# A 3x3 convolution rewritten as F(4,3) over rows and five products per two outputs over columns

## The chip, the cores and the metric

One core of a Trainium2 chip runs the whole program. The metric is device time in microseconds (us). Every figure "median" is over several executions; a profile is one execution, recorded instruction by instruction.

TensorE does matmuls (PE in the profile, PEld its weight loads), VectorE (DVE) and ScalarE (ACT) work element by element, GpSimd is POOL, SP issues transfers. SBUF and PSUM are the core's memories; the kernels' products land in PSUM.

## The reference

Two bottleneck blocks, one after the other, on 64 images of 1024 x 14 x 14, all float32:

```python
out = relu(bn(conv(x, w1, b1, 1, 0)))      # 1x1, 1024 -> 256
out = relu(bn(conv(out, w2, b2, 1, 1)))    # 3x3, 256 -> 256, padding 1
out = bn(conv(out, w3, b3, 1, 0))          # 1x1, 256 -> 1024
out = relu(x + softplus(residual_scale) * out)
```

`bn` takes mean and variance over all images and pixels, so each convolution must be finished for all images before its result can be normalised. That makes stages: 1x1, 3x3, a Gram stage (it gets the statistics of the third convolution from the second moments of its input), then the last 1x1 together with the next block's first.

## The kernel before

The 3x3 convolution is direct. Per two images the normalised activations go into a zero-padded tile, and each of two output halves is the sum of 18 products (2 input halves x 9 taps) of 392 columns:

```python
def conv2(t, w2, par, aff, stats):
    ...                                    # pad <- relu(scale * y + shift), ScalarE
    for o in range(MS):                    # 2 output halves
        ps = psum_tile()
        for s in range(MS):                # 2 input halves
            for k, (i, j) in enumerate(TAPS):
                nc.tensor.matmul(ps..., w2[:, s, k, o, :], pad[:, s, :, i : i + H, j : j + W],
                                 start=..., stop=...)
        y = ys[t][:, o, :]
        nc.scalar.activation(y, ps, AF.Identity, bias=...)      # PSUM -> SBUF
        nc.vector.bn_stats(stats[:, o, t, :], y)
...                                        # cut
for t in range(T):                         # T = 32 pairs of images
    conv2(t, w2, pb, aff, stats2)
aff = affine(aggregate(stats2, MS), MS, pb, G2, BE2)
grams = gram(aff, crow)                    # norm, transposes, Gram products
```

## Time and profile before

| | us |
|---|---|
| median of the kernel before | 3131.7 |
| TensorE busy (profiled run, span 3130.5) | 3088.2 |
| 3x3 products, both blocks | 1520.9 |
| 1x1 products, all | 1367.9 |
| VectorE busy, all stages | 563.9 |

The 1x1 figure is 681.2 + 686.7 from the two groups. The point to read from the table: one engine is busy for 99% of the span, and the direct 3x3 products are half of that. The column "mean ns" of a matmul group is how long one matmul is in flight; its cost in a stream is the distance from start to start, which is shorter.

### The profile page before, as it was taken

The numbers are of one execution on the slowest core, as the hardware profiler recorded it, in microseconds if no ns is written. First come the engines' busy times: TensorE is split into PE (matmuls) and PEld (weight loads), VectorE is DVE, ScalarE is ACT, GpSimd is POOL, SyncE is SP. The second block draws the span as 40 slices with busy tenths as digits, with TensorE's granted clock in tenths as the row PEclk, the third lists the DMA queues.
The fourth block names the chain that finished last, engine by engine and source line by source line (L and its number), as shares of the span: only waits on it lengthen the run. The fifth ranks groups of instructions, "written<-read, shape, count | busy, mean of one in ns | idle before, by whom it ended". The sixth has DMA issues, their size and how long they took to land.

```text
span 3130.5 us, 23038 instructions
## 1 busy us (share of the span) xinstructions
PE 3088.2 (99%) x10032; PEld 1845.2 (59%) x10032; DVE 563.9 (18%) x998; ACT 636.5 (20%) x1039; POOL 42.4 (1%) x76
## 2 busy tenths in 40 slices
PE   8999999999999999999999999999999999999998
PEld 5555555555555577555555555555555555875554
DVE  1111100000000033223222321000000000334444
ACT  1111111011111051223222321111101100524444
POOL 0000000000000000000000000000000000000000
PEclk9999999999999999999999999999999999999999
DMA  6444000000000021434344332000000000027886
GB/s 250 160 145 164 14 0 0 0 0 1 0 0 0 0 93 42 165 144 157 152 152 157 144 124 96 0 1 0 0 1 0 0 0 0 1 104 306 295 295 254
DMA packets 36581, 267.60 MB, mean 85 GB/s; under 512 B 2688, under 2 KB 2944, under 8 KB 27520
## 3 DMA queue, kind: packets, MB, share of 16 engines
q1 hardware_dynamic: 22592, 160.96, 14.4%
q0 software_dynamic: 13312, 102.76, 8.0%
q10 hardware_dynamic: 576, 2.40, 0.2%
q8 instruction: 79, 1.29, 0.2%
q14 instruction: 22, 0.18, 0.0%
HBM read 163.35 MB, written 102.76 MB: 85 GB/s over the span
## 4 chain that ended last, share of the span: by engine, by line
PE 59%; issue 39%; POOL 1%; DMA 1%; DVE 0%; POOLq 0%; ACT 0%; SPq 0%; ACTq 0%
PE ps L120 24%; PE ps L99 21%; PE ps L132 11%; PE g L151 1%; PE ps L163 1%; PE g L152 1%; POOL out L229 1%; DMA x<-mid 0%; DMA x<-in_x 0%; PE ps L209 0%; PE ps L206 0%; PE ps L197 0%; PE ps L199 0%; PE ps L198 0%; POOLq L229 0%
## 5 line engine op out<-in xcount | busy, mean ns | idle before, releaser
L120 PE MATMUL ps<-pad,w 128*128 128x392 f32 x4608 | 1520.9, 493 | 10.3 <-ACT pad L111 10.3
L120 PEld LDWEIGHTS ps<-pad,w 128*128 128x128 f32 x4608 | 872.5, 189 | 658.7 <-ACT pad L111 11.5
L99 PE MATMUL ps<-x,w 128*128 128x392 f32 x2048 | 681.2, 493 | 10.4 <-DMA x<-in_x 10.4
L132 PE MATMUL ps<-y,w 128*128 128x392 f32 x2048 | 686.7, 496 | 0.0
L99 PEld LDWEIGHTS ps<-x,w 128*128 128x128 f32 x2048 | 390.0, 190 | 295.9 <-issue 11.9
L132 PEld LDWEIGHTS ps<-y,w 128*128 128x128 f32 x2048 | 391.9, 192 | 286.6 <-issue 4.7
L227 ACT ACTIVATE x<-x,shift 128x392 f32<-128x392 f32 x512 | 318.2, 621 | 381.0 <-DVE x L224 381.0
L224 DVE SCALAR_TENSOR_TENSOR x<-ps,scale,x 128x392 f32<-128x392 f32 x512 | 320.3, 626 | 336.1 <-PE ps L132 332.4
L127 DVE BATCH_NORM_STATS2 stats<-y 128x6 f32<-128x392 f32 x128 | 72.9, 569 | 1450.2 <-ACT y L126 1450.2
L126 ACT ACTIVATE y<-ps,par 128x392 f32<-128x392 f32 x128 | 75.1, 587 | 1048.0 <-PE ps L120 1048.0
L104 ACT ACTIVATE y<-ps,par 128x392 f32<-128x392 f32 x128 | 75.1, 587 | 575.6 <-PE ps L99 575.6
L105 DVE BATCH_NORM_STATS2 stats<-y 128x6 f32<-128x392 f32 x128 | 72.9, 570 | 614.5 <-ACT y L104 614.5
L111 ACT ACTIVATE pad<-y,shift,scale 128x392 f32<-128x392 f32 x128 | 90.1, 708 | 320.0 <-PE ps L120 316.7
L151 PE MATMUL g<-zt 128*128 128x257 f32 x392 | 119.7, 387 | 0.0
L165 DVE TENSOR_TENSOR zt<-ps,crow 128x512 f32<-128x512 f32 x98 | 67.9, 693 | 108.5 <-PE ps L163 108.3
L152 PEld LDWEIGHTS g<-zt 128*128 128x128 f32 x392 | 75.2, 192 | 11.4
L139 ACT ACTIVATE y<-y,shift,scale 128x392 f32<-128x392 f32 x128 | 77.7, 701 | 3.2 <-DVE shift L266 3.2
L152 PE MATMUL g<-zt 128*128 128x129 f32 x392 | 76.3, 277 | 0.0
L163 PE MATMUL ps<-ident,y 128*128 128x128 f32 x392 | 61.8, 282 | 10.4 <-issue 5.2
L151 PEld LDWEIGHTS g<-zt 128*128 128x128 f32 x392 | 60.6, 195 | 0.6 <-DVE zt L165 0.6
L163 PEld LDWEIGHTS ps<-ident,y 128*128 128x128 f32 x392 | 47.7, 146 | 12.8 <-ACT y L139 7.0
L229 POOL DMA_DIRECT2D mid<-x x32 | 17.2, 537 | 1864.2 <-ACT x L227 1864.2
(65 smaller groups left out, 125.2 us busy)
## 6 DMA issues: line engine op xcount, KB each, us to landing
x<-in_x SPq DMA_DIRECT2D x64, 1568.0 KB, 6.4
mid<-x POOLq DMA_DIRECT2D x32, 1568.0 KB, 5.4
x<-mid SPq DMA_DIRECT2D x32, 1568.0 KB, 7.7
out<-x POOLq DMA_DIRECT2D x32, 1568.0 KB, 7.8
w<-in_w SPq DMA_DIRECT2D x2, 2304.0 KB, 15.5
w<-in_w ACTq DMA_DIRECT2D x2, 1024.0 KB, 5.9
w<-in_w SPq DMA_DIRECT2D x2, 1024.0 KB, 14.3
par<-in_par ACTq DMA_DIRECT2D x2, 146.5 KB, 10.2
```

The source lines that it names most:

```text
L99: nc.tensor.matmul(ps.rearrange("p (i f) -> p i f", i=G), w1[:, s, o, :], xt[:, :, s, :], start=(s == 0), stop=(s == CS - 1),)
L104: nc.scalar.activation(y, ps, AF.Identity, bias=par[:, B1 + o : B1 + o + 1])
L111: nc.scalar.activation(pad[:, s, :, 1 : H + 1, 1 : W + 1], ys[t][:, s, :].rearrange("p (i h w) -> p i h w", i=G, h=H), AF.Relu, bias=shift ...
L120: nc.tensor.matmul(ps.rearrange("p (i h w) -> p i h w", i=G, h=H), w2[:, s, k, o, :], pad[:, s, :, i : i + H, j : j + W], start=(s == 0 an ...
L126: nc.scalar.activation(y, ps, AF.Identity, bias=par[:, B2 + o : B2 + o + 1])
L132: nc.tensor.matmul(ps, w3[:, s, o, :], ys[t][:, s, :], start=(s == 0), stop=(s == MS - 1))
L139: nc.scalar.activation(y, y, AF.Relu, bias=shift[:, s : s + 1], scale=scale[:, s : s + 1])
L151: nc.tensor.matmul(g0, zt[:, c, 0:P], zt[:, c, :], start=first, stop=last)
L152: nc.tensor.matmul(g1, zt[:, c, P:M], zt[:, c, P:], start=first, stop=last)
L163: nc.tensor.transpose(tp[:, (c * MS + s) * P : (c * MS + s + 1) * P], y_all[:, s, px], ident)
L224: nc.vector.scalar_tensor_tensor(v, ps.rearrange("p (i f) -> p i f", i=G), scale[:, o : o + 1], v, ALU.mult, ALU.add)
L227: nc.scalar.activation(v, v, AF.Relu, bias=shift[:, o : o + 1])
```

## The change

The intent is to do the 3x3 convolution with fewer multiplications. Over rows, F(4,3) turns four output rows, each with three taps, into six products of combined input rows with combined filters (six in place of twelve). Over columns, two neighbouring outputs take five products in place of six: one product of w1 with the sum of an even and an odd column serves both outputs. In exchange VectorE forms the row combinations and the column sums, and recombines products into output rows. The combined filters are made on the chip in the first stage, kept in DRAM and fetched per use. SBUF pools are opened and closed by stage to make room.

```diff
+GI = 8                          # images of one group
+BUFS = dict(u=3, t=3, r=4, sums=4, ms=3, f=2)
+    def combine(g, pair):        # rows of products (1,2), (3,4) or (0,5)
+            if pair[0] == 1:
+                ...              # t1, t2: four scalar_tensor_tensor, two edge rows on ScalarE
+                nc.vector.tensor_add(ra, t1, t2)
+                nc.vector.tensor_sub(rb, t1, t2)
+            ...                  # cut: the other two pairs
+            for i, r in zip(pair, (ra, rb)):
+                nc.vector.tensor_add(sums, r[:, :, :, WH:], r[:, :, :, :WH])
+                u = pool.tile([P, MS, NK, M], FP, tag="u", name="u", bufs=BUFS["u"])
+                nc.sync.dma_start(out=u, in_=us[b][i])
+    def products(made):
+            ...                  # per row combination i and output half o, s = 0, 1:
+                        nc.tensor.matmul(m[:, o, :n], w(s, D1D2), sums[:, s]...)
+                        nc.tensor.matmul(odd, w(s, D1), r[:, s, :, WH:], ...)
+                        nc.tensor.matmul(odd[:, :, : WH - 1], w(s, D3), r[:, s, :, WH + 1 :], ...)
+                        nc.tensor.matmul(even, w(s, D2), r[:, s, :, :WH], ...)
+                        nc.tensor.matmul(even[:, :, 1:], w(s, D0), r[:, s, :, : WH - 1], ...)
+                ...              # ms <- m, ScalarE
+    def columns(done):           # f <- PSUM + ms, VectorE
+    def finish(g, pair, done, acc):
+            ...                  # output rows from f, then eight bn_stats per group
+        for k, (g, pair) in enumerate(pairs):
+            if pair[0] == 1 and g + 1 < NG:
+                norm(g + 1, aff)
+            now, ahead = ahead, combine(*pairs[k + 1]) if k + 1 < len(pairs) else None
+            acc = finish(g, pair, products(now), acc)
-        for t in range(T):
-            conv2(t, w2, pb, aff, stats2)
```

The host packs pixels in another order (8 images together, even and odd columns apart); the 1x1 stages keep their matmuls.

## The prediction

> **What bounds the kernel now.** I read the page first (busy shares), then the chain that ended last in order of time, then busy time by stage, then the groups by shape, and last single stretches of the timeline for what one instruction costs.
>
> ```profile
> PE 3088.2 (99%) x10032; PEld 1845.2 (59%) x10032; DVE 563.9 (18%) x998; ACT 636.5 (20%) x1039; POOL 42.4 (1%) x76
> PEclk9999999999999999999999999999999999999999
> ```
> TensorE is busy for 99% of the span at full clock; nothing else is above 20%. A change pays only where it shortens TensorE's queue, and only until another engine fills up.
>
> The chain in order of time (start, length, what), around the first 3x3 convolution:
> ```profile
> 349.51 0.59 ACT y L104
> 350.13 0.58 DVE stats L105
> 350.73 1.03 DVE mv L238
> 353.88 0.72 ACT pad L111
> 354.65 760.69 PE ps L120 x2304
> 1115.34 5.21 issue
> ```
> The 3x3 convolution of one block is 760.7 us of matmuls without a hole, 330.2 ns each (760.69/2304), with some 5 us of TensorE idle before it and 5.2 after it. By stage (window: length, then busy time and count of PE, PEld, DVE, ACT, POOL, clock, DMA share, GB/s):
> ```profile
> 0.00:340.00 340.00, 329.64 (x996) 190.27 (x997) 37.94 (x89) 39.67 (x68) 2.59 (x12) 1.00 0.45 166
> 340.00:1110.00 770.00, 764.82 (x2318) 438.72 (x2317) 41.75 (x79) 81.59 (x131) 0.00 (x0) 1.00 0.01 2
> ```
> In the 3x3 stage VectorE works 42 of 770 us and the DMA rings are empty: room for both kinds of work that the change brings. The costs of one instruction (busy us in total, mean ns):
> ```profile
> L120 PE MATMUL ps<-pad,w 128*128 128x392 f32 x4608 | 1520.9, 493 | 10.3 <-ACT pad L111 10.3
> L111 ACT ACTIVATE pad<-y,shift,scale 128x392 f32<-128x392 f32 x128 | 90.1, 708 | 320.0 <-PE ps L120 316.7 <-DVE shift L266 3.3
> L139 ACT ACTIVATE y<-y,shift,scale 128x392 f32<-128x392 f32 x128 | 77.7, 701 | 3.2 <-DVE shift L266 3.2
> L152 PE MATMUL g<-zt 128*128 128x129 f32 x392 | 76.3, 277 | 0.0
> L105 DVE BATCH_NORM_STATS2 stats<-y 128x6 f32<-128x392 f32 x128 | 72.9, 570 | 614.5 <-ACT y L104 614.5
> L165 DVE TENSOR_TENSOR zt<-ps,crow 128x512 f32<-128x512 f32 x98 | 67.9, 693 | 108.5 <-PE ps L163 108.3
> ```
> Mean ns of a matmul is a latency; its cost is the step from start to start. There are 4608 records for 2304 products in the code: each float32 product is two instructions. In the chain, 32 of 392 columns take 10.53 us (329.1 ns each), the Gram pairs of 257 columns 0.44 us (220 each), and pairs of 512 columns 0.86. All fit columns x 0.8333 ns + 2.5 ns. The timeline shows whether the weight load sets a floor:
> ```profile
> 1215.45 3.66 PE L206 MATMUL ps<-zmean,w 128*128 128x2 f32 x32
> 1228.67 0.17 DVE L253 TENSOR_TENSOR q<-r 128x8 f32<-128x8 f32 x1
> 1228.87 0.17 DVE L254 TENSOR_TENSOR q<-q,v 128x8 f32<-128x8 f32 x1
> ```
> 32 matmuls of two columns need 3.49 us by the chain, 109 ns each, so a fresh 128x128 weight set can go in every 109 ns; the 189 ns printed for a weight load is latency too. The two VectorE lines depend on each other and step 0.20 us; independent ones elsewhere in that stretch step 0.07 to 0.12.
>
> **What the Trainium skill says.** "TensorE: Matmul & The Clock Gate", Back-to-back issue gap, gives columns/2.4 + 2.5 ns warm, and LDWEIGHTS columns/1.2 (107 ns). The trace agrees on the 2.5 and on the load (109), but a float32 instruction takes twice the slope. "VectorE: DVE Perf Modes", section on the TRN2 errata, has a float32 tensor_tensor at (N+151)/0.96 ns: 691 for 512, measured 693; two-tensor float32 operations get no faster mode. "ScalarE: Activation LUTs", What ACT_TABLE_LOAD costs, has 280 + 0.833 N ns with one pointer operand and 93 more for a second: 700 for 392 elements, measured 701. "PSUM — Partial Sum Buffer", Specifications, warns that any non-contiguous pattern "slows matmuls significantly"; all outputs of the kernel before are contiguous, so no run shows it yet.
>
> **The change, part by part** (per group of 8 images; 8 groups per block, 16 in all).
>
> TensorE, removed: 144 products of 392 columns, 1521.4/16 = 95.1 us. Added: six transformed rows, each for two output halves with ten products: six of 224 columns and four of 192 (lines of 7 columns, 32 lines; the edge products drop one of 7). That is 2 x 2112 columns; the sixth row has 24 lines, 2 x 1584. In all 5 x 4224 + 3168 = 24288 columns, against 56448. Two instructions each: 48576 x 0.8333 = 40.48 us, plus 240 x 2.5 ns = 0.60: **41.1 us**. The smallest, 144 columns, takes 122.5 ns, above the 109 ns floor, so weight loads do not bind. All 16 groups: 657 us.
>
> VectorE, added: I count elements and instructions in the code. Row combinations 4032 + 4032 + 3472 elements (24 instructions), column sums out of PSUM 5152 (12), output rows 1792 + 4928 + 1568, and statistics 3136 (20 together): 28112 elements, 56 instructions. At 0.96 per ns: 29.3 us. With 65 ns for each step that overlaps and about seven dependent steps at 130 more: 33.8 us. With every instruction at its full 160 ns and 40 ns to the next: 40.5 us. So VectorE is 82 to 98% of TensorE's 41.1: full, but below it.
>
> ScalarE: two norms of 1568 elements (373 + 1306 ns, 3.4 us), five edge rows (about 0.4 each), seven PSUM copies (0.45 to 0.57 each): about 9 us. Hidden.
>
> DMA: six filter tiles of 1.31 MB per group, 7.9 MB per 41 us = 191 GB/s; the last stage of the kernel before (2870 to 3130 us) moves 286. Of three buffers the current pair holds two; the second tile of the next pair can be fetched when the first row is done with its own (7.1 us of products) and is needed 14 us later, and a 1.57 MB tile lands in 6.4 us now. Hidden. Filter preparation: 4 x about 12 us of VectorE, 15.7 MB of stores, in the first stage, where VectorE is at 38 of 340 us: hidden.
>
> At the two edges of each block TensorE is idle longer. Entry: now one pad of 0.72 us after the shift; then two norms (3.3), edge rows (0.4), two of the first combinations after the second norm (0.9), the sum and difference (2.1) and the first column sum (0.5), 7.2: +6.5 us. Exit: now one eviction, one statistic, and a norm; then the last row's columns (1), two output rows (1.8), eight statistics (3.9), two norms instead of one (+2.5): about +9 us. Two blocks: +31. The other stages keep their matmuls: the 1x1 convolutions have the same columns in another pixel order, their reads and evictions in runs of 28 or more, and the input tiles become one contiguous run per partition. I give that nothing either way.
>
> Sum: 3132 - 1521 + 657 + 31 = 2299. The windows of three pairs are uneven: while TensorE runs the short pair (12.5 us), VectorE must finish the columns, differences and rows of the middle pair and combine the next group's first pair, 11.4 us by the lower count and over 13 by the upper. I allow 1.5 us of stall per group, 24 us, giving 2323; I say 2325.
>
> **Rivals.** (a) VectorE becomes the bound of the stage. For: 40.5 of 41.1 us in the upper count, six hand-overs a group, one queue in order. Against: independent steps overlap in the trace. At 45 us a group the stage is 720: about 2390. (b) Short runs slow the matmuls: operands in runs of 6 or 7, outputs of 6 out of 7. For: the skill's warning. Against: runs of 14 in the input cost 330.2 against 329.1 ns here. If only the 16 shortened instructions per row took double, 16 x 162 ns x 6 x 16 = 250 us more: about 2570. (c) False waits between rows of the one big activation tile: ScalarE's norm of the next group (3.3 us) waiting for VectorE, and VectorE for it, once a group: +50, about 2375. (d) Weight tiles through DRAM arrive late: I see 1 to 2 us a tile at worst, 100 to 200 us more; the empty rings speak against it.
>
> **Range and chances.** The gain of 807 us rests on a TensorE rate measured to a per cent; a, c and half of b all push up, and almost nothing pushes below 2285 except the stall allowance and the edges being smaller. So the range is lopsided: 2285 to 2430. For a loss, the new stage would have to take over 95 us a group, more than twice the larger count; faster by over 2% 0.985, within 2% 0.01, slower 0.005.
>
> **What would show it.** After: 3840 instructions of the new products (240 x 16) in place of 4608; steps of about 189 ns (224 columns) and 162 (192) in the chain; a 3x3 stage of some 340 us with TensorE over 93% busy and VectorE at 80 to 95%; few waits of TensorE on the row combinations or on PSUM. If TensorE waits mostly on VectorE's sums, (a) holds; if 192-column steps exceed 165 ns, (b); if the filter tile releases it, (d). My prediction fails most simply if the overlap of VectorE instructions seen with 8 elements is not there with hundreds.

## The result, and the profile after

The changed kernel takes 2309.93 us in the median (4 runs, 2309.51 to 2311.61) against 3131.7 (3131.13 to 3132.34). The ratio is 0.7377, with a 95% interval of 0.7364 to 0.739. Ratios are the mean time of one kernel's fast runs over that of the other's of the same rounds, so they are not quite the ratio of the medians. The result is correct. The prediction was 2325, range 2285 to 2430.

The page of the changed kernel, busy time by engine and, in 40 slices, the clock granted to TensorE in tenths of full speed (PEclk; 9 is 90% or more):

```profile
PE 2236.0 (97%) x9264; PEld 1637.6 (71%) x9264; DVE 1077.3 (47%) x1854; ACT 581.4 (25%) x911; POOL 48.4 (2%) x102
PEclk9999998999998999999999999999999998999999
```

TensorE lost 852 us of work and is still busy for 97%. VectorE's work has nearly doubled. The clock now dips to 8 in three slices; the first two (346 to 404 and 692 to 750 us) hold the entry and the exit of the first 3x3 stage, which matters below.

The first block's 3x3 stage in three windows (length, then busy time and count of PE, PEld, DVE, ACT, POOL, clock, DMA share, GB/s): the entry, the products, the exit.

```profile
349.16:361.85 12.69, 0.01 (x2) 0.03 (x1) 8.59 (x21) 10.37 (x11) 0.00 (x0) 0.58 0.78 310
361.85:696.20 334.35, 334.35 (x1920) 331.76 (x1920) 260.72 (x430) 57.60 (x105) 0.00 (x0) 1.00 0.48 177
696.20:707.23 11.03, 0.03 (x1) 0.03 (x1) 8.55 (x22) 2.04 (x3) 0.20 (x4) 0.65 0.78 306
```

The middle line carries the answer: 1920 matmuls fill 334.35 of 334.35 us. VectorE is busy for 260.7 of them (78%), the DMA rings for half. The other two lines are the price: 12.7 and 11.0 us in which TensorE does nothing and VectorE and ScalarE, in turn, finish one stage and begin the next.

What TensorE waits for in the whole changed kernel (us in total, times, longest):

```profile
PE ps L334 <- ACT y L147: 23.6, 4, 11.0
PE ps L221 <- ACT t L161: 12.7, 1, 12.7
PE ps L221 <- DVE sums L201: 12.5, 1, 12.5
PE ps L136 <- DMA w<-in_w: 10.4, 1, 10.4
```

L221 is the first product of a row combination. It waits twice, once per block, at the entry, and never inside a stage. L334 are the Gram stage's transposes, after the exit. There is no wait for a filter tile, a PSUM bank or a row combination.

How fast the products step, from the timeline (start, length, engine, line, operation, count):

```profile
499.76 0.93 PE L226 MATMUL ps<-r,u 128*128 128x224 f32 x4
500.52 0.82 PE L228 MATMUL ps<-r,u 128*128 128x192 f32 x4
501.19 0.93 PE L232 MATMUL ps<-r,u 128*128 128x224 f32 x4
501.95 0.83 PE L234 MATMUL ps<-r,u 128*128 128x192 f32 x4
502.62 0.73 PE L221 MATMUL ps<-sums,u 128*128 128x224 f32 x3
```

Read the starts. Four instructions of 224 columns take 0.76 us (190 ns each), four of 192 take 0.67 (167.5 each). By the fit of the kernel before (0.8333 ns per column + 2.5 ns) they should be 189.2 and 162.5. The starts are printed to 10 ns, so four steps give a mean to some 2.5 ns only. The mean over all such steps at full pace in the trace is finer: 191.5 ns for the 224 columns of L226 and L232, which read runs of 7, 188.8 for the contiguous ones of L221, and 165.4 and 166.2 ns for the shortened ones of L228 and L234, which read runs of 6. The contiguous ones fit; runs of 7 are 2 ns over, runs of 6 are 3 to 4.

Two groups of the other engines (busy us in total, mean ns, idle before):

```profile
L147 ACT ACTIVATE y<-y,shift,scale 128x1568 f32<-128x1568 f32 x64 | 103.3, 1683 | 6.5 <-DVE shift L435 6.5
L270 DVE TENSOR_TENSOR fa<-f 128x896 f32<-128x896 f32 x16 | 17.4, 1084 | 0.0
```

ScalarE's norm of 1568 elements takes 1683 ns (the prediction's estimate was 1679), and a VectorE addition of 896 elements 1084 ns from its start to its end.

### The profile page after: what moved, and what is told of

Same layout as the page of the kernel before. It is cut to its first block, busy times and chain, and to the rows that moved or that the text cites. A ratio compares the mean times of both kernels' runs of the same rounds, so it can differ in the third digit from the quotient of the medians.

```text
span 2307.8 us, 22580 instructions
## 1 busy us (share of the span) xinstructions
PE 2236.0 (97%) x9264; PEld 1637.6 (71%) x9264; DVE 1077.3 (47%) x1854; ACT 581.4 (25%) x911; POOL 48.4 (2%) x102
## 5 line engine op out<-in xcount | busy, mean ns | idle before, releaser
L305 PE MATMUL ps<-y,w 128*128 128x392 f32 x2048 | 686.2, 496 | 0.0
L305 PEld LDWEIGHTS ps<-y,w 128*128 128x128 f32 x2048 | 392.0, 192 | 286.0 <-issue 4.4
L141 DVE BATCH_NORM_STATS2 stats<-y 128x6 f32<-128x392 f32 x128 | 71.6, 567 | 497.9 <-ACT y L138 497.9
L138 ACT ACTIVATE y<-ps,par 128x392 f32<-128x392 f32 x128 | 74.2, 587 | 557.5 <-PE ps L136 516.7
L221 PE MATMUL ps<-sums,u 128*128 128x224 f32 (+1 forms) x768 | 172.1, 347 | 25.2 <-ACT t L161 12.7
L254 DVE TENSOR_TENSOR f<-ps,ms 128x448 f32<-128x448 f32 x192 | 113.4, 602 | 147.0 <-PE ps L234 79.6
L226 PE MATMUL ps<-r,u 128*128 128x224 f32 (+1 forms) x768 | 173.6, 347 | 0.0
L232 PE MATMUL ps<-r,u 128*128 128x224 f32 (+1 forms) x768 | 172.5, 346 | 0.0
L221 PEld LDWEIGHTS ps<-sums,u 128*128 128x128 f32 x768 | 137.4, 190 | 26.6 <-ACT t L161 13.3
L228 PE MATMUL ps<-r,u 128*128 128x192 f32 (+1 forms) x768 | 153.5, 321 | 0.0
L234 PE MATMUL ps<-r,u 128*128 128x192 f32 (+1 forms) x768 | 153.3, 321 | 0.0
L226 PEld LDWEIGHTS ps<-r,u 128*128 128x128 f32 x768 | 141.8, 191 | 1.3
L245 ACT ACTIVATE ms<-ps 128x448 f32<-128x448 f32 (+1 forms) x80 | 41.9, 524 | 390.5 <-PE ps L221 390.5
L232 PEld LDWEIGHTS ps<-r,u 128*128 128x128 f32 x768 | 136.3, 188 | 1.4
L228 PEld LDWEIGHTS ps<-r,u 128*128 128x128 f32 x768 | 132.5, 189 | 1.1
L234 PEld LDWEIGHTS ps<-r,u 128*128 128x128 f32 x768 | 131.9, 188 | 0.9
L322 PE MATMUL ps<-zt 128*128 128x257 f32 x392 | 119.6, 387 | 0.5 <-DVE zt L336 0.5
```

Source lines behind the costliest of these rows:

```text
L138: nc.scalar.activation(y, ps.rearrange("p (h l) -> p h l", h=H), AF.Identity, bias=par[:, B1 + o : B1 + o + 1])
L221: nc.tensor.matmul(m[:, o, :n], w(s, D1D2), sums[:, s].rearrange("p l c -> p (l c)"), start=(s == 0), stop=(s == MS - 1),)
L226: nc.tensor.matmul(odd, w(s, D1), r[:, s, :, WH:], start=(s == 0), stop=False)
L228: nc.tensor.matmul(odd[:, :, : WH - 1], w(s, D3), r[:, s, :, WH + 1 :], start=False, stop=(s == MS - 1))
L232: nc.tensor.matmul(even, w(s, D2), r[:, s, :, :WH], start=(s == 0), stop=False)
L234: nc.tensor.matmul(even[:, :, 1:], w(s, D0), r[:, s, :, : WH - 1], start=False, stop=(s == MS - 1))
```

## The experiments

Eleven edits of the changed kernel and the changed kernel itself went to the chip. The theory: inside the 3x3 stage TensorE's columns are the only bound, the other engines and the DMA have slack, and what remains is at the edges. The rivals are those of the prediction.

### The control

The changed kernel again, on the chip and in the rounds of three later kernels. Expected:

> The changed kernel again, as the control on the same chip as the next three. All theories: 2308 to 2314.

Measured: 2311.62 us (6 runs, 2310.33 to 2312.46), ratio 0.738. One and the same program thus differs by some 2 us from call to call; its profile had 2239.1 us of TensorE work in place of 2236.0. Most of that lies in the clock's way back after idle time. The first 1x1 products need some 6 us until they step at their full pace, where the first trace has 3, and after the first 3x3 entry the granted clock stays at 0.50 for 4.7 us in place of 3.1. Each such microsecond costs about half of one, some 2.4 us in these two places, and the profiled spans differ by 2.9 (2310.7 and 2307.8). Differences under 3 us between calls are not read as effects below.

### Six plain products in place of five

```diff
-  m   += w(D1D2) * (even + odd)         # sum product
-  odd += w(D1) * even + w(D3) * even'   ; even += w(D2) * odd + w(D0) * odd'
+  odd  = w(D0) * even + w(D1D2) * odd  + w(D3) * even'
+  even = w(D3) * odd  + w(D1D2) * even + w(D0) * odd'
-  VectorE: sums, f <- PSUM + ms
+  ScalarE: f <- PSUM
```

> Undoes one half of the change: F(4,3) over rows stays, but the columns are computed with six plain products per two outputs in place of five and a sum; right result. TensorE per group: 29440 columns x 2 x 0.8333 = 49.1 us + 288 x 2.5 ns + 96 shortened instructions x 5 ns = 50.3 us against 41.7 (measured), so +8.5 x 16 = +137 us: about 2445 (2435 to 2455). VectorE loses the sums (3.1 us) and the additions out of PSUM (6.2 us): about 24.6 us a group. Rival (VectorE or its hand-overs set the pace of the stage): the stage gets shorter or stays, 2310 or less.

Measured: 2449.59 us (4 runs), ratio 0.7821, correct. That is 139.7 us above the first measurement of the changed kernel, where 137 was expected. One group of it:

```profile
407.00:457.30 50.30, 50.30 (x289) 49.73 (x288) 24.40 (x38) 8.59 (x17) 0.00 (x0) 1.00 0.43 157
```

TensorE is full for 50.3 us (expected 50.3); VectorE has fallen from 33.9 to 24.4 us and it bought nothing. The pace of the stage is TensorE's count of columns. The run also splits the gain. The rows alone, with plain columns, bring 682 of the 822 us (3131.7 - 2449.6); the five-for-six columns bring the other 140.

### Filters without DRAM traffic

```diff
-  u = pool.tile(...); nc.sync.dma_start(out=u, in_=us[b][i])     # per group and row
+  u = kept(i % 3)                                                 # three tiles, loaded once
```

> Wrong result on purpose: three filter tiles are loaded once per block and used for all six rows, so 96 loads of 1.31 MB become 6 and the DMA rings are empty in the 3x3 stage. My theory (the loads are hidden): 2306 to 2314. Rival (filter tiles arrive late or disturb the other engines): shorter by over 10 us, up to 100.

Measured: 2311.5 us (4 runs), ratio 0.7378; wrong result. The same stretch of the first stage without and with the traffic, this run first:

```profile
404.00:445.72 41.72, 41.72 (x243) 41.45 (x242) 33.90 (x57) 5.14 (x12) 0.00 (x0) 1.00 0.00 1
```

and the changed kernel:

```profile
404.00:445.72 41.72, 41.72 (x243) 41.45 (x242) 33.90 (x58) 5.14 (x12) 0.00 (x0) 1.00 0.52 191
```

Taking away 191 GB/s leaves every other number as it was. The filter transfers are hidden.

### More work for VectorE

```diff
+            for _ in range(n):                       # n = 1, 3, 5
+                nc.vector.tensor_add(new("spare"), ra, ra)
```

One, three and five unused additions per row pair, so 3, 9 and 15 us per group. Expected of one:

> One more VectorE addition of 896 elements per row pair (result unused), 1.0 us each in steps, so 3 us more per group of 8 images: 33.9 -> 36.9 us of VectorE against 41.7 us of TensorE. My theory (TensorE alone bounds the 3x3 stage, VectorE has room to spare): no change, 2305 to 2315 us, TensorE with no wait on VectorE inside the stage. Rival (the hand-overs of the row pairs are already at their limit, above all in the short third pair): up to 48 us longer, about 2330 to 2358.

Of three:

> Three more such additions per pair, 9 us more per group: 33.9 -> 42.9 us of VectorE, now above TensorE's 41.7. My theory: VectorE takes over as the bound of the stage, at least 1.2 us a group (19 us in all), and more because the three pairs are uneven: 2330 to 2400, with TensorE waiting on sums or on row combinations. If the count of VectorE's work as steps (elements/0.96 ns + 65 ns) is too high by more than 10 per cent, it stays at 2310.

Of five:

> Five more VectorE additions per pair, 15 us a group. The run with three more had VectorE in a period of 42.15 us a group (453.07 to 495.22 us) beside TensorE's 41.8, busy without a gap, and still no TensorE wait inside the stage. Theory (VectorE's queue is the only second limit, and buffers take up all unevenness): a period of 48.2 us a group, so 16 x 6.4 = 102 us longer: 2400 to 2420. Rival (the additions run in time that the earlier doses show as busy but that is not used, for instance because steps overlap further): under 2350.

Measured: 2313.99, 2313.96 and 2390.59 us (4 runs each; ratios 0.7386, 0.7388, 0.7632), all correct. With one addition nothing happens but 1 us more at each entry, which is the addition itself in the first pair. With three I had expected at least 2330, and missed. With five I had expected 2400 to 2420, and it stayed below. The group of the run with three, from the end of one output row to the next, and that of the run with five:

```profile
453.07:495.22 42.15, 42.15 (x246) 41.88 (x245) 42.12 (x66) 5.14 (x12) 0.00 (x0) 1.00 0.53 192
```

```profile
461.26:509.30 48.04, 42.12 (x232) 41.17 (x231) 48.04 (x73) 5.04 (x12) 0.00 (x0) 0.96 0.44 164
```

In the first, both engines are busy all the time: TensorE, the first busy time, for 42.15 of 42.15 us, and VectorE, the third, for 42.12. VectorE has no pause left and TensorE doesn't wait once. In the second VectorE sets the period, 48.04, as expected, and TensorE is idle for 5.9 of it. Its waits say on what (one of the 25, of 13.5 us, is the second block's entry):

```profile
PE ps L223 <- DVE sums L203: 66.1, 25, 13.5
```

So the steps were counted well, but the limit was put too low. Part of a block's VectorE work lies outside the products: the first combinations come before the first product, the last columns and statistics after the last. With five additions the first block's products run from 363.28 to about 737.5 us, 374 us, while eight periods are 8 x 48.04 = 384. So some 10 us per block lie outside; this figure is taken from this run and tested on the other. With three, 8 x 42.15 = 337, less 10 is 327, and TensorE's own 334 still hides it. VectorE becomes the bound near (334 + 10)/8 = 43 us a group, not at 41.7; these two figures are worked out, not run. In the run with five, the products of a block take 374 - 334 = 40 us more, 80 in all, and the time is 79 over the control (2390.59 - 2311.62), so the whole loss lies in there. Of the first block's 40 us, 27.0 are waits on the sums; in most of the rest the products step slower, since the granted clock falls after these waits (0.96 in the period above).

### Which side of a shortened product is slow

Two looks, both with wrong results. One makes the output of the 192-column products contiguous, the other their input:

```diff
-  odd[:, :, : WH - 1]                   # output: 6 of every 7
+  eo[:, 0, : lines * (WH - 1)]          # output: contiguous
```
```diff
-  r[:, s, :, WH + 1 :]                  # input: runs of 6
+  sums[:, s]...[:, : lines * (WH - 1)]  # input: contiguous
```

> Wrong result on purpose: the shortened products (192 or 144 columns) write a contiguous PSUM range in place of 6 of every 7 elements; they read the same runs of 6. In the changed kernel four such instructions of 192 columns step 0.67 us (167.5 ns each) where 192 x 0.8333 + 2.5 = 162.5. If the gaps in the output cost the 5 ns: 0.65 us for four, TensorE's 1920 instructions of a block in about 330.5 us in place of 334.4. If the runs of 6 in the input cost it: unchanged at 334.4.

> Wrong result on purpose: the shortened products read a contiguous range of the sums in place of runs of 6 of every 14; they still write 6 of every 7 elements. If the input runs cost the 5 ns per instruction: the 1920 instructions of a block take about 330.5 us in place of 334.4. If the output gaps do: unchanged at 334.4.

Measured: 2312.33 us with contiguous outputs, 2306.12 with contiguous inputs (one run each). The timeline of the run with contiguous outputs:

```profile
502.59 0.82 PE L228 MATMUL ps<-r,u 128*128 128x192 f32 x4
503.25 0.93 PE L232 MATMUL ps<-r,u 128*128 128x224 f32 x4
```

and of the run with contiguous inputs:

```profile
501.61 0.81 PE L228 MATMUL ps<-sums,u 128*128 128x192 f32 x4
502.26 0.93 PE L232 MATMUL ps<-r,u 128*128 128x224 f32 x4
```

Four steps of 192 columns take 0.66 us in the first (0.67 for L234 there) and 0.65 in the second. Over all steps at full pace in the traces the means are 165.4 ns (L228) and 166.2 (L234) with contiguous outputs, the same as in the changed kernel, and 162.1 and 161.9 with contiguous inputs, the fit's 162.5 within 1 ns. So the 3 to 4 ns belong to the way the input is read (the edit changes the tile along with the runs; I take it to be the runs, as runs of 7 are over too), and the gaps in the output cost nothing that shows. The first block's products took 335.1 and 332.7 us, 2.4 us over 768 shortened instructions, 3 ns each. The expectations, 330.5 for the side that costs and 334.4 for the other, were made with 5 ns, and the granted clock was at 0.50 for some 1.5 us longer at these entries than in the changed kernel's.

### The idle edges

What is left besides columns is the idle time around each 3x3 stage. Four attempts, each with a right result. The first trims the chain:

```diff
-  norm(0): both halves on ScalarE
+  norm(0): one half on ScalarE, the other on VectorE; in the Gram stage first rows 0 to 3
-  eight bn_stats after the last output row
+  bn_stats per class of output rows (k::4), two classes before the last products
-  if pair[0] == 1: norm(g + 1)
+  if pair[0] == 3: norm(g + 1)
```

> An attempt to beat the changed kernel where TensorE still waits, at the edges of the 3x3 stage (12.7 us before, 11.0 us after, in each block); right result. The first group's second half is normed on VectorE beside ScalarE, the next group's norm no longer stands in front of the first edge rows, the statistics are taken per output row class so that half of them are done before the last products, and the first norm of the Gram stage is cut at four rows. Theory: entry shorter by about 3 us, exit by about 5, so 16 us in all: 2294 (2288 to 2302). Rival (the idle at the edges overlaps waits for the filter or weight DMA, which then end last): under 4 us gained, 2306 or more.

Measured: 2299.78 us (5 runs), ratio 0.7343, inside the expected range. The exit fell from 11.0 to 7.1 us of idle; the entry only from 12.7 to 11.6. The order in an engine's queue need not be that of the code: in this run's trace ScalarE still takes the next group's norm (from 355.89 us) in front of the edge rows (357.48), although the code now asks for it later. So the entry gained 1 us of the 3 expected.

The second leaves the chain alone and fills the idle time with matmuls whose result nobody reads:

```diff
+  keep_warm(16)       # after each 1x1 stage: products of the identity with old activations
+  keep_warm(14)       # after each 3x3 stage
```

> The changed kernel plus matmuls whose result nobody reads, 16 products after each 1x1 stage and 14 after each 3x3 stage, sized to run about 10 and 9 of the 12.7 and 11.0 us in which TensorE is idle there; right result. Theory: part of what an idle edge costs is the granted clock falling (0.58 to 0.65 in those stretches, and the first 20 products' instructions after the entry take 5.2 us in place of 3.6); kept busy, each of the four edges gets 1.5 to 3 us cheaper: 6 to 12 us, 2298 to 2304. Rival (the slow start is the filter tiles' or sums' arrival, not the clock): no gain, 2308 to 2314.

Measured: 2302.05 us (4 runs), ratio 0.7349, against the control's 2311.62 in the same rounds: 9.6 us less for doing more. The first products of the stage in the changed kernel:

```profile
361.85 1.83 PE L221 MATMUL ps<-sums,u 128*128 128x224 f32 x4 [12.68 <-ACT t L161]
363.47 1.63 PE L226 MATMUL ps<-r,u 128*128 128x224 f32 x4
364.94 0.82 PE L228 MATMUL ps<-r,u 128*128 128x192 f32 x4
```

and with the filling (L305 is here the filling):

```profile
350.22 10.77 PE L305 MATMUL ps<-y,ident 128*128 128x392 f32 x32 [0.77 <-ACT y L138]
362.02 0.99 PE L221 MATMUL ps<-sums,u 128*128 128x224 f32 x4 [1.04 <-issue]
362.86 0.93 PE L226 MATMUL ps<-r,u 128*128 128x224 f32 x4
```

After 12.7 idle us the first four instructions take 1.62 us (361.85 to 363.47), twice their 0.76; after 1.0 idle us they take 0.84. The Trainium skill, "TensorE: Matmul & The Clock Gate", Part 1, says that an idle window of some 3.4 us drops the array to half its clock, and that it needs about as long at work to come back. This agrees on the half, and roughly on the times. From 351.3 us, some 2 us after the last 1x1 product, to 364.9, some 3 us after the first 3x3 product, the granted clock of the changed kernel is half:

```profile
351.30:364.90 13.60, 3.05 (x8) 2.82 (x9) 10.20 (x24) 11.55 (x13) 0.00 (x0) 0.50 0.63 267
```

From 364.94 us on the products step at full pace.

The third puts both together and mends the entry's order:

```diff
+  first group's edge rows on VectorE; first column sum ahead of the difference
+  keep_warm(12), keep_warm(8)
```

> The trimmed edges (2299.8 us, entry 11.6 and exit 7.1 us of idle) with two mends and the filling matmuls: the first group's edge rows on VectorE, because ScalarE had put the second group's norm before them, and the first column sum ahead of the difference; 12 and 8 filling products. Right result. Theory: entry 1.7 us shorter and the clock kept: 2 x (1.7 + 1.6 + 2.5) = 12 us less than 2299.8: 2288 (2284 to 2293). Rival as for the filling matmuls alone: 2296 or more.

Measured: 2293.93 us (4 runs), ratio 0.7324; just above the expected range. The entry was not shorter (350.33 to 362.22): the built queue still had the difference before the sum. The clock was kept at the first block's entry, but not at the second's, where TensorE was idle for 3.05 us after the filling:

```profile
1495.06 1.83 PE L241 MATMUL ps<-sums,u 128*128 128x224 f32 x4 [3.05 <-issue]
1496.68 1.70 PE L246 MATMUL ps<-r,u 128*128 128x224 f32 x4
```

The first 16 instructions take 5.85 us there (1495.06 to 1500.91), twice their time at full pace. At the first entry, after 3.0 us of idle, they did not slow down.

The fourth goes round this on TensorE's side:

```diff
-  products of the first pair: sum product first
+  products of the first pair: sum product last
```

> As the run before (2293.9 us), but in the first pair of each block TensorE takes the sum products last, so it can start from the first combined row, before the difference and the column sums. There VectorE's queue had the difference ahead of the first sum although the code asked for the other order, and the entry stayed at 11.9 us (350.33 to 362.22). Right result. Theory: TensorE starts when the first row is done, 1.7 us sooner in each block, 3 us in all: 2290.5 (2288 to 2292.5). Rival (the start waits for the first filter tile from DRAM instead): no gain, 2293 to 2295.

Measured: 2287.14 us (5 runs, 2286.39 to 2289.68), ratio 0.7301 (0.7291 to 0.7311), on another chip than the run before it; just below the expected range. The entry is now 350.31 to 360.67, so 1.5 us shorter, and as much in the second block. There the idle time after the filling has halved, and the products start at full pace:

```profile
1492.00 1.00 PE L247 MATMUL ps<-r,u 128*128 128x224 f32 x4 [1.51 <-issue]
1492.84 0.82 PE L249 MATMUL ps<-r,u 128*128 128x192 f32 x4
```

The second block's products take 2.8 us less for that. So the traces account for the 5.9 us between the two profiled spans (2293.2 and 2287.3): 3.1 from the two entries, 2.8 from the clock. The medians differ by 6.8; the rest is within the drift between calls. It is the fastest version: 1% below the changed kernel, whose own ratio to the kernel before is 0.7377 to 0.738.

## Why the prediction was right, point by point

The prediction's sum was 2323, given as 2325; measured 2309.93. That it is only 0.6% off is in part luck: the products took 13 us more than it said, and the edges 3 and the stalls 24 less. Without the stall allowance, which had the wrong mechanism, it would have been 11 us too low.

**TensorE's columns, 657 us.** Right in kind, 1.9% too small. The two blocks' products took 334.35 and 335.48 us, 669.8; the second block's line:

```profile
1503.04:1838.52 335.48, 335.48 (x1920) 332.74 (x1920) 260.84 (x430) 57.72 (x105) 0.00 (x0) 0.99 0.48 177
```

Of the 13 us above, about 5 are the runs of 6 (1536 instructions at some 3 ns), about 3.5 the runs of 7 (as many at some 2.3 ns), and about 4 the clock, a cost that the prediction did not count: it is at 0.50 for the first 3.1 us of the one block's products and the first 5.3 of the other's, and half of that is lost. The weight loads did not bind, although loads are in flight for 331.8 of 334.4 us: with contiguous inputs and as many loads the smallest products (144 columns) step 122 ns, the 122.5 of the fit.

**VectorE, 33.8 to 40.5 us a group.** The lower count was right. In the changed kernel a period of 41.69 us holds 33.87 us of VectorE work. The overlap of steps that the prediction saw at 8 elements holds at 896: additions of 896 elements last 1.08 us and start 1.00 us apart, 896/0.96 + 65 ns. So rival (a) does not hold, and the additions show how far away it was: about 9 us of VectorE work per group.

**Stalls, 24 us.** This term was wrong: it measured zero. Inside the stages the profile has no TensorE wait at all. The reason given was the short third pair, in which VectorE should have had to fit 11.4 to 13 us into 12.5. The run with three additions shows that the unevenness is taken up: VectorE had no pause left, and TensorE still did not wait. That row buffers and work pulled ahead do it is my reading; no run changed the number of buffers. The expectation for three additions failed on the same point.

**Edges, 31 us.** 28. TensorE's waits around the two 3x3 stages rose from 20.7 us (10.3 + 5.2 + 5.2 in the profile before) to 48.8 (23.6 + 12.7 + 12.5). The entry (+7.5 where +6.5 was said) was longer than the prediction's sum by a norm and a subtraction that the built queues put in between, the exit (+6.6 where +9 was said) shorter, because the first of the two output rows was added before the last products were over (at 691.48 us) and the first transpose needs one norm only.

**Rivals (b), (c), (d).** (b) exists, at 3 to 4 ns per shortened instruction and not the doubling feared, and on the input side, not the output. The prediction's one reading on it, 330.2 ns for runs of 14 against 329.1, was not the runs: at full pace the steps of both are 329.2 ns in the mean over the trace of the kernel before, and its first 3x3 products ran at a granted clock of 0.50 for 4.1 us (354.65 to 358.7), which raises the mean. (c), false waits inside the activation tile, would have had to reach TensorE as waits inside the stage: there are none. (d) was refuted by taking the transfers away.

Put together from the traces: 3130.5 - 1521.4 + 669.8 + 28.1 = 2307.0, where the profiled run has 2307.8. The remaining 0.8 us I don't assign.

## What to carry to other kernels

When one engine is busy for 99%, count its work in its own unit (here columns) at the rate the trace shows; the new stage's length followed to 2% here. Count the other engines by start-to-start steps, not by printed durations: the durations would have called VectorE 98% full where it was 81%. After the big term is gone, look at the idle edges. An idle wait costs its length and then the clock's way back, and filling it with useless matmuls can be faster than leaving it.

## What the Trainium skill lacked or had wrong

- "TensorE: Matmul & The Clock Gate" has no time for float32 products ("FP8 and Floating Point Precision" counts four passes for true float32, which fits, but names no instructions and no time): in all kernels here each is two instructions of 0.8333 ns per column + 2.5 ns (392 columns: 329.2 ns).
- "PSUM — Partial Sum Buffer", Specifications, says that any non-contiguous pattern slows matmuls significantly. Float32 outputs of 6 in every 7 elements cost nothing that shows: 192-column instructions step 165.4 and 166.2 ns with gaps and without.
- "SBUF — State Buffer" has a penalty for each access that crosses to a new 16-byte line, but no page has a figure for short runs in a matmul's float32 input: runs of 6 cost 3 to 4 ns on 162.5, runs of 7 some 2 ns on 189.2, runs of 14 nothing that shows on 329.
- "VectorE: DVE Perf Modes", on the errata, sets 58 + N cycles against a measured duration and calls it too small. Here it fits the step from start to start of independent float32 additions: 896 elements, 1.00 us (954 cycles are 0.99), while the duration is 1.08.
